# The 65-key score tile of an fp32 attention kernel, computed in column tiles of TensorE's array

## The chip, the cores and the metric

The kernel runs on one core of a Trainium2 chip. Five engines work side by side and meet only at semaphores: TensorE (PE in the profile, with PEld for its weight loads), VectorE (DVE), ScalarE (ACT), GpSimd (POOL) and SyncE (SP, which issues most DMAs). The metric is the device time of one execution in microseconds. Before the change the two runs took 2556.80 and 2558.18 us, median 2557.49 us.

## What is computed

A gated cross-attention block is followed by a gated mixture of low-rank experts, all in fp32. What matters here is the attention, with 4 batches, 256 queries, 1601 keys, 32 query heads in 8 groups of 4 that share keys and values, and head size 128:

```python
q = (query @ Wq + bq).reshape(B, L, NKV, G, HDIM)        # B=4, L=256, NKV=8, G=4, HDIM=128
k_, v_ = jnp.split(kv @ Wkv + bkv, 2, axis=-1)           # 1601 keys
scores = jnp.einsum('blkgd,bmkd->bkglm', q, k) * scale
attn = jax.nn.softmax(scores, axis=-1)
o = jnp.einsum('bkglm,bmkd->blkgd', attn, v).reshape(B, L, NHEAD * HDIM)
return o @ Wo + bo
```

## The kernel before

**Tiles.** The scores are laid out with keys on the partitions and queries along the free dimension. The outer loop runs over the 32 pairs of batch and key head, and within each over two halves `l` of 128 queries: 64 groups. A group has 4 query heads times 128 queries, so 512 query columns (`W`). The 1601 keys are 12 tiles of 128 and one of 65 (`FULL` is the number of that last tile, `REST` is 65). `score_unit(key, j)` computes the scores of one entry of `pairs`: entry 0 is the 65-key tile alone, entries 1 to 6 are two full tiles each. So the 65-key tile opens every group.

**One score tile.** `kT` (128 head dimensions by the keys) is the stationary operand, `qT` (128 by 4 by 128 queries) is streamed, and the result goes to one of the 8 PSUM banks, 512 fp32 columns wide. In the trace each fp32 product stands as two passes, that is two weight loads and two matmul records. ScalarE then copies the bank into the SBUF tile `p` (L1151). `p` has a ring of buffers. A bank or a buffer of `p` can be written again when its reader is done.

**The softmax.** VectorE keeps a running maximum over the group's `p` tiles (`fold`, L1067 to L1073; the 65-key tile joins at L1070, when entry 2 is there). `softmax` reduces it over the partitions and queues the subtraction (VectorE, L1181), the exponential (ScalarE, L1184) and the sums (VectorE, L1073). `av_unit` multiplies the result with the values (L1233). Its first entry again is the 65-key tile, now with 65 rows of contraction.

**The order of the work.** It is written out by a planner at build time: `spend` advances TensorE's planned clock by a product's booked cost, `act` and `vec` those of ScalarE and VectorE, and `pump`, `fit` and `force` take queued pieces of softmax work when the planned clocks allow it. `run_group` puts the score products of one group between the value products of the group before, and `window` fills in projections (L896, L907), output products (L484, L1310) and transposes (L258). The booked costs do not enter the program as such; they only decide in which order each engine's instructions stand. `mm_cost(n)` books 2 * (max(n, 128) / 1.2 + 2) ns for one fp32 product of n columns.

**Two small places elsewhere** that the prediction reads: L238 transposes the biases with 48 rows of contraction, once; L258 transposes the router's weights with 8 rows of contraction, four times near the end. All other products of the kernel contract over 65 or 128 rows and write 65 or 128 partitions.

Of the kernel before, what the change touches and what calls it, by code (L numbers as in the profile page):

```python
# [15 lines left out]
P = 128  # L16
# [3 lines left out]
G = NHEAD // NKV  # L20
# [7 lines left out]
def flamingo_kernel(  # L28
# [51 lines left out]
    nc = tc.nc  # L80
# [8 lines left out]
    FULL = KT - 1 if rows[-1] < P else KT  # L89
    W = G * P  # L90
# [13 lines left out]
    REST = rows[-1] if FULL < KT else 0  # L104
# [13 lines left out]
    SEM = 200  # L118
# [3 lines left out]
    clock = {"now": 0.0, "v": 0.0, "a": 0.0, "hold": 0.0}  # L122
    free = [0.0] * NBANK
    done = {}
    queues = {q: deque() for q in ("sub", "oT", "so", "exp", "ln", "T", "norm", "sum", "low", "low_a")}

    def vec(ns, ready=None):

        clock["v"] = max(clock["v"], clock["now"] + SEM if ready is None else ready) + ns
        return clock["v"] + SEM  # L130

    def act(ns, ready=None):
        clock["a"] = max(clock["a"], clock["now"] + SEM if ready is None else ready) + ns
        return clock["a"] + SEM
# [5 lines left out]
    def start_of(piece):  # L140
        engine, _, ready, _, _ = piece
        if not isinstance(ready, float):
            ready = done.get(ready, NEVER)
        return max(clock[engine], ready)

    def take(q):

        piece = q.popleft()
        engine, ns, _, fn, key = piece
        start = start_of(piece)  # L150
        fn()
        clock[engine] = start + ns
        if key is not None:
            done[key] = start + ns + SEM + (GP_COPIES if key[0] == "part" and key[2] < 4 else 0)

    def pump(until=NEVER, most=None):

        n = 0
        while most is None or n < most:
            heads = [(start_of(q[0]), i, q) for i, q in enumerate(queues.values()) if q]  # L160
            if not heads:
                return n
            start, _, q = min(heads)
            if start == NEVER or start + min(q[0][1], 1200) / 2 > until:
                return n
            take(q)
            n += 1
        return n

    def force(key):  # L170


        while key not in done:
            q = next((q for q in queues.values() if any(p[4] == key for p in q)), None)
            if q is None:

                assert pump(most=1), key
                continue
            ready = q[0][2]
            if not isinstance(ready, float):  # L180
                force(ready)

            engine, start = q[0][0], start_of(q[0])
            for name, other in queues.items():
                fit = 1200 if name == "sub" else FIT
                while other is not q and other and other[0][0] == engine:
                    if start_of(other[0]) + other[0][1] > start + fit:
                        break
                    take(other)
            take(q)  # L190
        return done[key]

    def fit(engine, until):

        while True:
            some = [
                (start_of(q[0]), i, q)
                for i, q in enumerate(queues.values())
                if q and q[0][0] == engine and start_of(q[0]) + q[0][1] <= until + FIT
            ]  # L200
            if not some:
                return
            take(min(some)[2])

    def spend(ns, ready=0.0):

        clock["now"] = max(clock["now"], ready) + ns
        pump(clock["now"])

    def bank(name):  # L210
        free.remove(min(free))
        return ps.tile([P, 512], F32, tag="bank", name=name)

    give = free.append
# [32 lines left out]
    def mm_cost(n):  # L247

        return 2 * (max(n, P) / 1.2 + 2)
# [404 lines left out]
    def key_col(i):  # L654

        return HK if i == FULL else i * P + (REST if i * P >= HK else 0)
# [101 lines left out]
    qT_t, kT_t, v_t = {}, {}, {}  # L758
# [302 lines left out]
    def fold(acc, op, j, key):  # L1061


        p = p_t[key]
        first = NPAIR - FULL // 2
        if j == first + 1:
            nc.vector.tensor_tensor(acc, p[first], p[first + 1], op)  # L1067
            if first:
                r = rows[-1]
                nc.vector.tensor_tensor(acc[:r, 0, :], acc[:r, 0, :], p[0][:r, 0, :], op)  # L1070
                return 1930
        elif j > first + 1:
            nc.vector.tensor_tensor(acc, acc, p[j], op)  # L1073
        else:
            return 0
        return 1220

    def spread(acc, op, nm, res, after=None, eng=nc.vector):
# [31 lines left out]
            (710, back),  # L1110
        ]

    def score_unit(key, j):

        b, h, l = key
        nm = "_".join(map(str, key))
        free_p = 0.0
        if j == 0:
            p_t[key] = []
            acc_t[key] = pool.tile([P, 2, W], F32, tag="mx", name=f"mx_{nm}", bufs=1)  # L1120
        if key == last and j > 0:

            if j == 1:
                flat = pool.tile([P, NC * 2 * HW], F32, tag="ctxT", name="p_last", bufs=1)
                late.extend(
                    flat[:, i * 2 * W : (i + 1) * 2 * W].rearrange("p (t w) -> p t w", t=2)
                    for i in range(NPAIR - 1)
                )
            p = late.pop(0)
        else:  # L1130

            if len(ring) >= NBUF:
                before, i = ring[-NBUF]
                free_p = force(("sum", before, max(i, min(NPAIR - FULL // 2 + 1, NPAIR - 1))))
            ring.append((key, j))
            p = pool.tile([P, 2, W], F32, tag="p", name=f"p_{nm}_{j}", bufs=NBUF)
        p_t[key].append(p)
        for k, i in enumerate(pairs[j]):
            r = rows[i]
            spend(mm_cost(W), max(min(free), done.get(("qT", b, h), 0.0)))  # L1140
            sc = bank(f"sc_{nm}_{i}")
            nc.tensor.matmul(  # L1142
                sc[:r, :],
                kT_t[b, h][:, key_col(i) : key_col(i) + r],
                qT_t[b, h][:, :, l * P : (l + 1) * P],
                start=True,
                stop=True,
            )
            t = max(clock["now"] + SEM, free_p)
            fit("a", t)  # L1150
            nc.scalar.copy(p[:r, k, :], sc[:r, :])  # L1151
            t = act(585, t)
            give(t)
        fit("v", t)
        ns = fold(acc_t[key], ALU.max, j, key)
        if ns:
            vec(ns, t)
# [523 lines left out]
    def run_group(cur, prev, ahead=AHEAD, most=NC * TR_COST):  # L1681


        for j in range(NPAIR + ahead):
            if cur is not None and j < NPAIR:
                score_unit(cur, j)
                if j == NPAIR - 1 and cur[0] == B - 1 and cur[1] >= NKV - 2:
                    softmax(cur)
                short_tasks(most)
            if prev is not None and prev[2] == 0 and j > 2:  # L1690
                block_sums(prev, j >= NPAIR - 1)
            if prev is not None and j >= ahead:
                av_unit(prev, j - ahead)
                short_tasks(most)
        if cur is not None and not (cur[0] == B - 1 and cur[1] >= NKV - 2):
            softmax(cur)
# [173 lines left out]
    for hi, (b, h) in enumerate(heads):  # L1870
        pair, coming = (b, h // 2), next_pair(b, h // 2)
        nxt = heads[hi + 1] if hi + 1 < len(heads) else None
        for l in range(NL):
            now = hi * NL + l
# [99 lines left out]
```

## Time and profile before

| | value |
|---|---|
| runs | 2556.80 and 2558.18 us, median 2557.49 us |
| profiled execution, first to last instruction | 2555.5 us |
| TensorE's granted clock, mean | 1.000 |
| PE busy | 2547.3 us |
| DVE busy | 2202.6 us |
| ACT busy | 1188.1 us |
| 65-key score products (L1142, 128 matmul records) | 65.3 us |
| copies of the 65-key tile (L1151, 64 of them) | 37.2 us |
| mean traffic with HBM | 65 GB/s |

The profile is that of one execution. Busy times are unions, so overlapping records of one engine count once. A matmul record is longer than the distance to the next one because matmuls are pipelined: what a product costs TensorE is the distance between starts, not the length of its record. The profile is read on the engine that has no idle time, and for that engine by its distances.

### The profile page before, as it was taken

What the parts mean: (1) busy time and instruction counts of PE and PEld (TensorE: products, weight loads), DVE (VectorE), ACT (ScalarE), POOL (GpSimd) and SP (SyncE); (2) the same over time, 40 slices, a digit from 0 to 9 for tenths busy, and PEclk for the clock granted to TensorE, in tenths of its full rate; (3) what the DMA queues carried; (4) which work ended last, traced back from release to release, by engine and by line L of the source; (5) the groups of instructions that cost most, each with busy time, mean ns of one, the idle gap of its engine ahead of it and who ended that gap; (6) DMA issues with size and microseconds to landing.
All of it is one profiled execution on the core that took longest, in us unless ns stands there. A gap on an engine that the chain in (4) does not pass through costs nothing.

```text
span 2555.5 us, 26175 instructions
## 1 busy us (share of the span) xinstructions
PE 2547.3 (100%) x9235; PEld 1487.8 (58%) x9235; DVE 2202.6 (86%) x3310; ACT 1188.1 (46%) x1897; POOL 150.4 (6%) x401
## 2 busy tenths in 40 slices
PE   9999999999999999999999999999999999999999
PEld 7557566565555656455565665756656455555554
DVE  4889898899889989899788887878889899998897
ACT  3544454445434555455444444445454445544551
POOL 0000000000000000110000000000000000000000
PEclk9999999999999999999999999999999999999999
DMA  4313222324110111012121111212221011111000
GB/s 158 123 64 108 87 95 84 114 85 149 48 56 23 44 52 56 25 40 83 49 81 37 62 52 62 81 48 81 85 84 56 25 52 52 52 44 52 17 17 33
DMA packets 75499, 167.16 MB, mean 65 GB/s; under 512 B 5372, under 2 KB 32028, under 8 KB 72808
## 3 DMA queue, kind: packets, MB, share of 16 engines
q1 hardware_dynamic: 74424, 164.41, 19.3%
q8 instruction: 73, 1.20, 0.2%
q0 software_dynamic: 416, 0.81, 0.1%
q14 instruction: 58, 0.48, 0.1%
q10 hardware_dynamic: 528, 0.26, 0.0%
HBM read 119.06 MB, written 46.40 MB: 65 GB/s over the span
## 4 chain that ended last, share of the span: by engine, by line
PE 99%; DVE 1%; DMA 0%; ACT 0%; issue 0%; DVEq 0%; ACTq 0%
PE av L1233 28%; PE sc L1142 28%; PE pxk L896 6%; PE pxv L907 6%; PE pxq L896 4%; PE pyk L896 3%; PE pyv L907 3%; PE po L1310 3%; PE pox L484 3%; PE pyq L896 2%; PE pzk L896 2%; PE pzv L907 2%; PE poy L484 1%; PE pzq L896 1%; PE ptv L1020 1%; PE pk L803 1%
## 5 line engine op out<-in xcount | busy, mean ns | idle before, releaser
L1142 PE MATMUL sc<-qT,kT 128*128 128x512 f32 (+1 forms) x1664 | 775.9, 592 | 0.0
L1151 ACT COPY p<-sc 65x512 f32<-65x512 f32 x820 | 474.3, 586 | 636.5 <-PE sc L1142 575.2
L1233 PE MATMUL av<-p,v 65*128 65x512 f32 x1640 | 766.1, 592 | 1.2 <-ACT p L1184 1.2
L1233 PEld LDWEIGHTS av<-p,v 65*128 65x128 f32 x1640 | 309.5, 190 | 376.2 <-issue 370.8
L1142 PEld LDWEIGHTS sc<-qT,kT 128*128 128x128 f32 (+1 forms) x1664 | 307.0, 186 | 374.3 <-issue 340.4
L1181 DVE TENSOR_TENSOR p<-p,mb 65x512 f32<-65x512 f32 x442 | 485.9, 1137 | 0.1
L1184 ACT ACTIVATE p<-p 65x512 f32<-65x512 f32 x442 | 423.1, 990 | 38.6 <-DVE p L1181 34.5
L1073 DVE TENSOR_TENSOR mx<-mx,p 128x1024 f32<-128x1024 f32 x252 | 308.1, 1223 | 137.9 <-ACT p L1151 134.8
L1073 DVE TENSOR_TENSOR sm<-sm,p 128x1024 f32<-128x1024 f32 x252 | 307.4, 1220 | 9.8
L1090 POOL COPY quad_sm<-quad_sm 32x16 f32<-32x16 f32 x186 | 70.7, 380 | 2088.3 <-DVE quad_sm L1086 2083.1
L896 PE MATMUL pxq<-xq,wq 128*128 128x256 f32 x512 | 131.2, 379 | 0.0
L941 ACT ACTIVATE kT<-pxk,biasT 128x384 f32<-128x384 f32 (+1 forms) x120 | 57.9, 508 | 141.8 <-PE pxk L896 141.0
L896 PEld LDWEIGHTS pxq<-xq,wq 128*128 128x128 f32 x512 | 92.5, 189 | 31.2 <-issue 15.3
L941 ACT ACTIVATE qT<-pxq,biasT 128x256 f32<-128x256 f32 x64 | 30.3, 473 | 140.2 <-PE pxq L896 140.2
L944 ACT COPY v<-pxv 128x384 f32<-128x384 f32 x90 | 43.0, 477 | 104.8 <-PE pxv L907 104.8
L896 PE MATMUL pxk<-T,wk 128*128 128x417 f32 (+1 forms) x240 | 90.4, 499 | 0.0
L907 PE MATMUL pxv<-wv,T 128*128 128x128 f32 x720 | 90.2, 275 | 0.0
L896 PE MATMUL pxk<-ctxT,wk 128*128 128x417 f32 (+1 forms) x240 | 90.0, 499 | 0.0
L907 PE MATMUL pxv<-wv,ctxT 128*128 128x128 f32 x720 | 90.0, 275 | 0.0
L907 PEld LDWEIGHTS pxv<-wv,T 128*128 128x128 f32 x720 | 86.4, 192 | 4.7 <-issue 4.3
L907 PEld LDWEIGHTS pxv<-wv,ctxT 128*128 128x128 f32 x720 | 86.4, 192 | 4.7 <-issue 4.3
L1067 DVE TENSOR_TENSOR mx<-p,p 128x1024 f32<-128x1024 f32 x63 | 76.8, 1220 | 13.1 <-ACT p L1151 12.8
(264 smaller groups left out, 2809.6 us busy)
## 6 DMA issues: line engine op xcount, KB each, us to landing
wo<-in_L_xattn_Wo_dram SPq DMA_DIRECT2D x18, 1024.0 KB, 5.3
kept_q<-wq SPq DMA_DIRECT2D x16, 896.0 KB, 4.8
wq<-kept_q SPq DMA_DIRECT2D x16, 896.0 KB, 5.1
wo<-kept_wo SPq DMA_DIRECT2D x13, 1024.0 KB, 5.8
wk<-kept_k SPq DMA_DIRECT2D x11, 896.0 KB, 4.6
wv<-kept_v SPq DMA_DIRECT2D x11, 896.0 KB, 4.4
ctx<-in_ctx_dram SPq DMA_DIRECT2D x36, 256.0 KB, 2.7
wq<-in_L_xattn_Wq_dram SPq DMA_DIRECT2D x32, 256.0 KB, 3.1
```

Of the source, the lines that this page charges most:

```text
L484: nc.tensor.matmul(bk[:, :HD], left[i]()[:, c, :], blk[:, c, :], start=first and c == 0, stop=c == 1, skip_group_check=True,)
L896: nc.tensor.matmul(bk[:, :n], a(SLOT[i], c), operand(i, c, s, n), start=first and c == 0, stop=c == 1, skip_group_check=True,)
L907: nc.tensor.matmul(bk[:, t * HDIM : (t + 1) * HDIM], operand(i, c, s + t * P, P), a(SLOT[i], c), start=first and t == 0 and c == 0, stop=c ...
L941: nc.scalar.activation(dst, src, AF.Identity, bias=bias_of(kind, h0 + f))
L1067: nc.vector.tensor_tensor(acc, p[first], p[first + 1], op)
L1073: nc.vector.tensor_tensor(acc, acc, p[j], op)
L1142: nc.tensor.matmul(sc[:r, :], kT_t[b, h][:, key_col(i) : key_col(i) + r], qT_t[b, h][:, :, l * P : (l + 1) * P], start=True, stop=True,)
L1151: nc.scalar.copy(p[:r, k, :], sc[:r, :])
L1181: nc.vector.tensor_tensor(p, p, m, ALU.subtract)
L1184: nc.scalar.activation(p, p, AF.Exp, scale=scale)
L1233: nc.tensor.matmul(av, v_t[b, h][:r, i, :], p_t[key][j][:r, k, :], start=(j == 0 and k == 0), stop=(j == NPAIR - 1 and k == len(pairs[j]) ...
L1310: nc.tensor.matmul(po, oT_t[key][:, g, :], w_t["o", b, h][:, g, :], start=(g == 0), stop=(g == G - 1),)
```

## The change

The 65-key score tile is no longer one product of 65 keys by 512 queries. Its first 64 keys become two products of 256 queries each. The first writes partitions 0 to 63 of the bank and the second writes partitions 64 to 127, in the same 256 columns. The 65th key becomes four products of one key by 128 queries, which write partitions 0, 32, 64 and 96 of the next 128 columns of the same bank. In the built program the first two have the array shape 128 rows by 64 columns, the other four 128 by 32, and everything around them 128 by 128. Only the last of the six raises the semaphore, by 6.

ScalarE brings the pieces back into the old layout of `p`: two copies of 64 by 256 and four of 1 by 128 in place of one copy of 65 by 512. The first of them waits for all six products. The new function is called from `score_unit` for the tile `FULL`, in all 64 groups.

```diff
+    def split_scores(b, h, l, sc, p, free_p):
+        half, k0 = P // 2, key_col(FULL)
+        kT, qT = kT_t[b, h], qT_t[b, h]
+        for n in range(2):
+            nc.tensor.matmul(
+                sc[n * half : (n + 1) * half, : W // 2],
+                kT[:, k0 : k0 + half],
+                qT[:, 2 * n : 2 * n + 2, l * P : (l + 1) * P],
+                start=True, stop=True, skip_group_check=True,
+            )
+        for g in range(G):
+            nc.tensor.matmul(
+                sc[32 * g : 32 * g + 1, W // 2 : W // 2 + P],
+                kT[:, k0 + half : k0 + half + 1],
+                qT[:, g, l * P : (l + 1) * P],
+                start=True, stop=True, skip_group_check=True, tile_position=(0, 32 * g),
+            )
+        t = max(clock["now"] + SEM, free_p)
+        fit("a", t)
+        for n in range(2):
+            nc.scalar.copy(p[:half, n * W // 2 : (n + 1) * W // 2], sc[n * half : (n + 1) * half, : W // 2])
+            t = act(375, t)
+        for g in range(G):
+            nc.scalar.copy(p[half : half + 1, g * P : (g + 1) * P], sc[32 * g : 32 * g + 1, W // 2 : W // 2 + P])
+            t = act(265, t)
+        return t
...
         for k, i in enumerate(pairs[j]):
             r = rows[i]
+            if i == FULL and REST == P // 2 + 1:
+                spend(mm_cost(W // 2) + mm_cost(P) + 200, max(min(free), done.get(("qT", b, h), 0.0)))
+                sc = bank(f"sc_{nm}_{i}")
+                t = split_scores(b, h, l, sc, p[:, k, :], free_p)
+                give(t)
+                continue
             spend(mm_cost(W), max(min(free), done.get(("qT", b, h), 0.0)))
```

The planner books 848 ns of TensorE for the tile in place of 857, and about 3 us of ScalarE in place of 0.8. So it also places other work differently. On TensorE a few projection and output products change places with their neighbours, on ScalarE and VectorE exponentials, sums and maxima move by some places, and four DMAs move past one neighbour each: three on SP's queue (two copies of query weights to HBM, L337, go ahead of a load of output weights, L424; one load of kept output weights, L421, ahead of another, L375) and one on POOL's (the bias load, L601, ahead of a small copy, L1097). ScalarE loads its function table twice more (once at L287, once at L1184). Apart from these two, no instruction is added or removed but those of the 65-key tile.

## The prediction

> **What bounds the kernel now.** I read the page first, then TensorE's groups by shape, then short stretches of the timeline. The page:
>
> ```profile
> span 2555.5 us, 26175 instructions
> PE 2547.3 (100%) x9235; PEld 1487.8 (58%) x9235; DVE 2202.6 (86%) x3310; ACT 1188.1 (46%) x1897; POOL 150.4 (6%) x401
> PEclk9999999999999999999999999999999999999999
> PE 99%; DVE 1%; DMA 0%; ACT 0%; issue 0%; DVEq 0%; ACTq 0%
> ```
>
> TensorE has no idle time worth the name (2555.5 - 2547.3 = 8.2 us), at full clock, and it is 99% of the chain that ended last. So each nanosecond that the change adds to TensorE's stream shows in the span, and each that it takes away does too, until VectorE (86%) or another engine has to be waited for. The span stands 2.0 us under the median of the runs (2557.49 us); I add the change to the median.
>
> Then the groups by shape: count, busy us, mean record ns, idle before.
>
> ```profile
> L1142 PE MATMUL sc<-qT,kT 128*65 128x512 f32 x128 | 65.3, 592 | 0.0
> L1151 ACT COPY p<-sc 65x512 f32<-65x512 f32 x64 | 37.2, 581 | 58.7 <-PE sc L1142 57.5 <-DVE sm L1073 1.0
> L856 ACT COPY v<-pv 128x256 f32<-128x256 f32 x12 | 3.9, 375 | 11.8 <-PE pv L847 11.8
> L1549 ACT COPY ffn_w<-pmt 128x128 f32<-128x128 f32 x6 | 1.6, 266 | 27.1 <-PE pmt L1544 27.1
> ```
>
> The first is what the change replaces: 64 products in two passes each. A record is 592 ns long, but passes overlap, so their price has to be read as a distance between starts. The timeline gives it (start us, us, what; a run of equal records is one row):
>
> ```profile
> 60.57 1.03 PE L896 MATMUL pxq<-xq,wq 128*128 128x256 f32 x4
> 61.43 1.88 PE L1142 MATMUL sc<-qT,kT 128*65 128x512 f32 x4
> 2395.11 1.50 PE L907 MATMUL pyv<-wv,T 128*128 128x128 f32 x12
> ```
>
> A pass of 512 columns takes (1.88 - 0.592) / 3 = 0.429 us, one of 256 (61.43 - 60.57) / 4 = 0.215, and one of 128 (1.50 - 0.275) / 11 = 0.111, with 0.275 the length of its record. So time goes with the columns streamed, and the weight load beside it is free as long as it is fetched while the pass before streams.
>
> **What the new shapes cost in themselves.** The change leaves the array's 128 x 128 shape in every group. Before does this twice in the whole run, with fewer rows (48 at L238, 8 at L258); with fewer columns it never does.
>
> ```profile
> 9.69 0.60 PE L258 MATMUL pt_ctx<-ident,ctx 128*128 128x128 f32 x4
> 10.21 0.26 PE L238 MATMUL pb<-ident,bias 48*128 48x48 f32 x1
> 10.40 0.66 PE L258 MATMUL pt_ctx<-ident,ctx 128*128 128x128 f32 x4
> ...
> 2417.58 1.02 PE L1142 MATMUL sc<-qT,kT 128*128 128x512 f32 x2
> 2418.53 0.41 PE L258 MATMUL pt_base<-ident,base 8*128 8x8 f32 x4
> 2418.87 1.12 PE L1233 MATMUL av<-p,v 128*128 128x512 f32 x2
> ```
>
> At 9.69 four transposes 0.11 apart should let the next start at 10.12; it starts at 10.21, 0.09 late. That one product then holds the stream 0.19 where 0.06 to 0.11 would do (0.08 to 0.13 too long), and the four after it take 0.66 and not 0.60, because the first had to wait for its own weights (0.06). In all 0.23 to 0.28 us for going in and out. The other place: due at 2417.58 + 2 x 0.429 = 2418.44, started 2418.53 (0.09); its four products are (0.41 - 0.20) / 3 = 0.07 apart, so the last ends its turn at 2418.81 and the next starts at 2418.87 (0.06); and two value passes take 1.12 and not 1.02 (0.10 for exposed weights). In all 0.25. So a change of shape costs 0.06 to 0.13, and the first weights after it 0.06 to 0.10 for 128 columns.
>
> **The sum, part by part.**
>
> *Removed:* two passes of 0.429 = 0.859 us per group.
>
> *Streaming added.* Four passes of 256 and eight of 128. If none lies beside another: 4 x 0.215 + 8 x 0.111 = 1.75 us. If everything that the words promise lies beside each other: 2 x 0.215 + 2 x 0.111 = 0.65. Between them is what I expect. A product's two passes stand next to each other in the stream, records start in the program's order in every row I read, and the second pass of a product uses the same columns of the array as its first. So the first pass of the second column tile can at best run beside the second pass of the first tile, and n tiles take n + 1 slots. That is 3 slots of 0.215 and 5 slots of 0.111: 0.645 + 0.555 = 1.20. Side by side therefore never gets below the 0.859 that it replaces.
>
> *Starting a column tile.* The trace has no two products in different column tiles. The nearest small distance is the 0.07 above; the other end is nothing. There are 1 + 3 such steps per group: 0 to 0.28, I take half, 0.14. The Trainium skill, "TensorE: Matmul & The Clock Gate", section "Measured speedup vs the span model", puts a step between tiles at about 4 ns, which would make this term an estimate of 0.016 and the forecast some 8 us less; no run here shows it.
>
> *Changes of shape:* three per group (into 64 columns, into 32, back to 128). In 0.09 twice, out 0.06 to 0.13, exposed weights 0.10 after the way out and 0.02 to 0.05 after each way in (fewer columns are loaded): 0.34 to 0.51; I take 0.44. The floor for the range is 0, since these rows change the rows of the array and not its columns. The Trainium skill, "TensorEngine Tiling (Array Packing)", section "Tiling Modes", says that changing the mode, not just the tile, drains TensorE; it gives no price, and speaks against a change that does so three times for 65 keys.
>
> *Sum on TensorE:* 1.20 + 0.14 + 0.44 = 1.78 against 0.859: 0.92 us per group, 64 groups, 59 us.
>
> *ScalarE.* Two copies at 375 ns (the 128x256 row) and four at 266 (the 128x128 row) replace one of 581: 2 x 375 + 4 x 266 - 581 = 1233 ns per group, 79 us in all, and two more table loads of 1.28 us. I cost them at nothing: the work that hides them is TensorE's own, since ScalarE is idle 54% of the span and in the row of the 128x512 copies alone waits 517.7 us for scores. Behind the six copies in ScalarE's queue stand the copies of entry 1, and then VectorE's maximum, which takes entry 0 only after entries 1 and 2. With 0.859 per score product and 586 ns per copy, ScalarE regains 0.27 us a tile, more where value products lie between; the bank of the 65-key tile is one of 8. If that cover were gone, up to 79 us would be added.
>
> *The planner.* TensorE is booked 9 ns less, so the plan is near the old one; on SP's queue three DMAs of about 1 MB stand one place earlier, and each lets its neighbour wait for 5 to 6 us (its time to landing); on POOL's the bias load does the same to a small copy. The busiest queue fills 19.3% of the DMA engines, and TensorE waits for none of these in this trace. Price 0, with the 8.2 us of present idle as the scale for either sign.
>
> **Rivals.**
>
> 1. *Nothing runs side by side* (each pass streams alone, whatever its columns). 1.75 + 0.44 = 2.19, +1.33 a group, +85: 2643 us. For it: no row shows two passes in parallel. Against: only the change's own intent, which is no evidence, so I weigh it high.
> 2. *Weights are no longer fetched ahead in column tiles.* Twelve passes each pay 0.05 (half the columns) to 0.10: 2.79 to 3.39, +124 to +162: 2681 to 2720. For: it happens at each change of shape above. Against: in one shape it happens nowhere; the four 8-row products are 0.07 apart.
> 3. *Everything side by side, shape changes priced as above:* 0.65 + 0.44 = 1.09, +15: 2572 us.
> 4. *The other side: everything side by side and shape changes free.* 0.65 against 0.859, 0.20 us saved a group: 2544 us. It decides where three changes cost less than 0.20 together, 0.07 each; the two rows say 0.06 to 0.13 plus weights, and the order of the passes speaks against it too.
> 5. *ScalarE becomes late,* and entry 0's copies hold up banks: up to 79 us on top of the forecast, 2696. Against: its idle time above.
>
> **How the numbers follow.** Forecast 2557.5 + 59 = 2617 us, chance 0.56. Its own range: low with 0 and 0.34 (1.54, +44: 2601), high with 0.28 and 0.51 (1.99, +72: 2630). Rival 1 has 0.22, rival 2 0.07, rival 3 0.08, rival 4 0.05, rival 5 0.02. The range of 2572 to 2646 holds the forecast and rivals 1 and 3, also side by side in order with free changes of shape (1.20, +22); it leaves out rivals 2, 4 and 5, 0.14, and what little lies outside the forecast's own range. A difference of 2%, about what a measurement of this kernel can tell from no change, is 51 us, or 1.66 us for the new tile. Seven tenths of the forecast's cases lie above that, all of rivals 1, 2 and 5, none of 3 and 4: 0.39 + 0.31 = 0.70, which I lower to 0.67 since the border runs through the likeliest case. Faster by 2% would need 0.80 of the 0.859 us saved: 0.01. Within 2%: 0.32.
>
> **What would show it.** In the trace after: the first pass of the second 256-column product starting with the second pass of the first (0.22 after the start, not 0.43) shows the staggered order; four single-key products taking 0.56 and not 0.89 show the same. The wait ahead of the first 64-column pass, of the first single-key pass and of the next full product's second pass give the three changes. ScalarE's busy time should rise by some 80 us with TensorE's idle time still near 8 us; if that rises by tens, rival 5 was right. I am wrong if the distance from the first split pass to the next full score pass is not between 1.5 and 2.0 us.

## The result, and the profile after

The changed kernel takes 2577.59 us (2576.85 and 2578.32), 20.1 us more than before: ratio 1.0076, 95% interval 1.0047 to 1.0105. The forecast was 2617 us. So it is slower, as forecast, but by a third of the forecast amount. It lies inside the stated range of 2572 to 2646 us only because that range also held rival 3; the forecast's own range began at 2601, and slower by more than 2%, to which I had given 0.67, did not come (it is 0.8%).

The page of the kernel after, the lines that answer to those shown of before:

```profile
span 2575.1 us, 27764 instructions
PE 2563.0 (100%) x9875; PEld 1485.5 (58%) x9875; DVE 2205.2 (86%) x3310; ACT 1259.8 (49%) x2219; POOL 144.7 (6%) x401
PE 99%; DVE 1%; ACT 0%; DMA 0%; issue 0%; SPq 0%; ACTq 0%; DVEq 0%
```

The span grew by 19.6 us. TensorE's busy time grew by 15.7 us of this, and its idle time by the rest (2575.1 - 2563.0 = 12.1 us, 8.2 before). These are two separate effects. The first is in the new tile. Its groups by shape, and one group in the timeline:

```profile
L1118 PE MATMUL sc<-qT,kT 128*64 128x256 f32 x256 | 41.7, 405 | 0.0
L1125 PE MATMUL sc<-qT,kT 128*1 128x128 f32 x512 | 25.6, 271 | 0.0
...
1504.55 0.81 PE L484 MATMUL pox<-xa,xa 128*128 128x256 f32 x3
1505.29 0.65 PE L1118 MATMUL sc<-qT,kT 128*64 128x256 f32 x4
1505.87 0.40 PE L1125 MATMUL sc<-qT,kT 128*1 128x128 f32 x8
1506.20 1.56 PE L1176 MATMUL sc<-qT,kT 128*128 128x512 f32 x3
```

In the last four rows the first number is the start in us, the second the time to the end of the row's last record. Read as in the prediction, by distances. The three output passes (`pox`) start 0.215 apart, the last at 1504.98, so the next is due at 1505.19; it starts at 1505.29. Four passes of 256 columns then lie within 0.65 us, of which 0.38 is the length of the last record. So the last one started only 0.27 after the first; four in a row would have put it at 0.65 or later. The eight single-key passes start within 0.40 - 0.27 = 0.13. From the first split pass to the next full one it is 0.91 us (1506.20 - 1505.29). I had set 1.5 to 2.0 as the bounds outside of which I would be wrong.

The exact record starts are the same to a few ns in all 64 groups. I call *tile time* the distance from when the first split pass was due to where the next full product would have started with its weights ready (the start of its second pass less 0.4295 us). Its median is 1.109 us; before it was 0.859:

| piece of the tile time | us |
|---|---|
| late start of the first split pass | 0.093 |
| two slots of 256 columns | 0.431 |
| weights of the first pass, not fetched ahead | 0.052 |
| from 64 columns to 32, beyond the slot | 0.100 |
| two slots of 128 columns | 0.216 |
| from 32 columns to 128, beyond the slot | 0.113 |
| weights of the next full product | 0.104 |

The three changes of shape have one price. Counted from where the last pass of the old shape ends its slot, in whichever column tile it is, the next pass starts 0.093 us later in all three; the 0.100 and 0.113 hold besides it the one and the three steps of 0.007 by which the last column tile started behind the first. In all ten profiles with narrow shapes this price is 0.093 to 0.095 (medians).

64 x (1.109 - 0.859) = 16.0 us. This is, to 0.3 us, the growth of TensorE's busy time. The other 4 us are in the list of what TensorE waited for (engine, line, what for: us, times, longest):

```profile
PE av L1267 <- ACT p L1218: 3.3, 2, 1.6
PE sc L1176 <- ACT p L1185: 1.4, 1, 1.4
PE warm L1829 <- DVE ones L1826: 1.1, 1, 1.1
PE pt_ctx L258 <- DMA ctx<-in_ctx_dram: 1.0, 1, 1.0
```

Before, the corresponding list had one wait for an exponential and none for a score copy:

```profile
PE av L1233 <- ACT p L1184: 1.2, 1, 1.2
```

Two waits on ScalarE are new. One is a value product that waits for an exponential (1.63 us at 2490.58), the other a score product that waits for a bank (1.43 us at 1105.53).

### The profile page after: what moved, and what is told of

The parts are those of the page before. It is cut to its first block, busy times and chain, and to the rows that moved or that the text cites. A ratio compares the mean times of both kernels' runs of the same rounds, so it can differ in the third digit from the quotient of the medians.

```text
span 2575.1 us, 27764 instructions
## 1 busy us (share of the span) xinstructions
PE 2563.0 (100%) x9875; PEld 1485.5 (58%) x9875; DVE 2205.2 (86%) x3310; ACT 1259.8 (49%) x2219; POOL 144.7 (6%) x401
## 4 chain that ended last, share of the span: by engine, by line
PE 99%; DVE 1%; ACT 0%; DMA 0%; issue 0%; SPq 0%; ACTq 0%; DVEq 0%
PE av L1267 28%; PE sc L1176 26%; PE pxv L907 6%; PE pxk L896 6%; PE pxq L896 4%; PE po L1344 3%; PE pyk L896 3%; PE pyv L907 3%; PE pox L484 3%; PE pyq L896 2%; PE pzk L896 2%; PE pzv L907 2%; PE sc L1118 1%; PE poy L484 1%; PE pzq L896 1%; PE ptv L1020 1%
## 5 line engine op out<-in xcount | busy, mean ns | idle before, releaser
L1176 PE MATMUL sc<-qT,kT 128*128 128x512 f32 x1536 | 727.8, 597 | 1.4 <-ACT p L1185 1.4
L1185 ACT COPY p<-sc 128x512 f32<-128x512 f32 x756 | 431.3, 588 | 519.6 <-PE sc L1176 445.3
L1176 PEld LDWEIGHTS sc<-qT,kT 128*128 128x128 f32 x1536 | 284.8, 190 | 346.5 <-issue 315.8
```

The source lines that it names most:

```text
L1176: nc.tensor.matmul(sc[:r, :], kT_t[b, h][:, key_col(i) : key_col(i) + r], qT_t[b, h][:, :, l * P : (l + 1) * P], start=True, stop=True,)
```

## The experiments

The theory after the result: passes in different column tiles stream together whenever their tiles are free, so the tile streams for 0.65 us and pays 0.46 for three changes of shape; the other 4 us come from the order of other work or from ScalarE's extra copies. Each experiment takes one of these apart. The diffs are against the changed kernel; `...` stands for lines left out. Times are medians, each beside runs of before on the same chip (median 2557.3 to 2558.5 us). Tile times are read from the record starts as above.

### Same width, one column tile (same_tile)

```diff
-                sc[n * half : (n + 1) * half, : W // 2],
+                sc[:half, n * W // 2 : (n + 1) * W // 2],
...
-                sc[32 * g : 32 * g + 1, W // 2 : W // 2 + P],
+                one[:1, g * P : (g + 1) * P],
...
-                start=True, stop=True, skip_group_check=True, tile_position=(0, 32 * g),
+                start=True, stop=True, skip_group_check=True, tile_position=(0, 0),
```

`one` is a second bank; the copies, left out here, read from the new places.

> All six products of the 65-key tile stay as narrow as in the changed kernel, but every one goes to the first column tile of its shape (two banks instead of one). Theory, side by side: what makes the changed tile 1.11 us is that passes in different column tiles stream together (0.65 us) while three changes of shape cost 0.46. Without different tiles the passes stream one after another: 4 x 0.215 + 8 x 0.111 = 1.75, with 0.46 it is 2.21 us a group, 1.35 over the old tile, +87, with some 4 us of waits about 2648 us. Rival, narrow passes are cheap in themselves, whichever tile they lie in: the time stays at 2578 us.

2640.83 us, ratio 1.0326 (1.0311 to 1.0341). The timeline of one group:

```profile
865.12 1.08 PE L1118 MATMUL sc<-qT,kT 128*64 128x256 f32 x4
866.12 1.03 PE L1125 MATMUL one<-qT,kT 128*1 128x128 f32 x8
867.09 0.70 PE L1178 MATMUL sc<-qT,kT 128*128 128x512 f32 x1
```

The same four passes now take 1.08 us where they lay within 0.65, and the eight take 1.03 where they lay within 0.40. The tile time is 2.169 us, and 64 x (2.169 - 0.859) = 83.8 us against 83.5 measured. So the narrow passes are not cheaper in themselves here; it takes different column tiles for them to share the array. The expectation of 2648 us was 7 too high: 2.6 us is in the tile (2.21 for 2.169), and the new waits on ScalarE, 4 us, did not come in this run. This is also what the prediction's first rival would have looked like (2643 us).

### The order of the products (order)

```diff
         for n in range(2):
-            nc.tensor.matmul(
-                sc[n * half : (n + 1) * half, : W // 2],
-                kT[:, k0 : k0 + half],
-                qT[:, 2 * n : 2 * n + 2, l * P : (l + 1) * P],
+            for g in range(2):
+                nc.tensor.matmul(
+                    sc[n * half : (n + 1) * half, g * P : (g + 1) * P],
+                    kT[:, k0 : k0 + half],
+                    qT[:, 2 * n + g, l * P : (l + 1) * P],
...
```

> The 64 keys as four products of 128 queries: two in the first column tile, then two in the second. Theory, passes of different tiles are brought together however far apart they stand in the program: 4 x 0.111 = 0.44 for the four products, as much as the two of 256 take now: 2578 to 2580 us. Rival, only products that are neighbours in the program share the array: of the eight passes at most one pair lies side by side, 7 x 0.111 = 0.78, +0.35 a group over the changed kernel, +22: 2600 us; with none side by side 8 x 0.111 = 0.89, +29: 2607 us.

2579.09 us, ratio 1.0084 (1.0069 to 1.0099), tile time 1.121. In the group that starts at 845.08 the eight 64-column passes start at 0, 0.014, 0.160, 0.174, 0.269, 0.283, 0.379 and 0.392: four pairs. The two products for the second tile stand behind both products for the first in the program, and still each of their passes goes beside one of the first tile's. So two products need not be neighbours in the program to share the array.

### One shape less (two64)

```diff
-        for g in range(G):
+        for n in range(2):
             nc.tensor.matmul(
-                sc[32 * g : 32 * g + 1, W // 2 : W // 2 + P],
-                kT[:, k0 + half : k0 + half + 1],
-                qT[:, g, l * P : (l + 1) * P],
+                sc[n * half : (n + 1) * half, W // 2 :],
+                kT[:, k0 + half : k0 + 2 * half],
+                qT[:, 2 * n : 2 * n + 2, l * P : (l + 1) * P],
...
```

The four copies of the 65th key, left out here, read from the new places.

> The 65th key is computed in the 64-column shape as well: a slice of 64 keys that starts with it (the other 63 rows are not used) by 256 queries in each of the two column tiles. One change of shape fewer. Theory: 2 x 0.215 + 2 x 0.215 streaming, in 0.093 + 0.052, out 0.113 + 0.104: 1.22 us a group, 0.36 over the old tile, +23, with 4 us of waits 2585 us. Rival, the 0.10 us ahead of the single-key products is not the change of shape but theirs whatever the shape (new weights, another part of the bank): 1.32 us, 2591 us.

2588.26 us, ratio 1.0120 (1.0105 to 1.0135).

```profile
1312.74 0.65 PE L1118 MATMUL sc<-qT,kT 128*64 128x256 f32 x4
1313.22 0.60 PE L1125 MATMUL sc<-qT,kT 128*64 128x256 f32 x4
```

The time, 3 us from either forecast, does not tell the two apart; the tile time does. It is 1.211, as expected by the theory (1.22) and not by the rival (1.32). The pairs start at 0, 0.267, 0.483 and 0.699: the last key's pairs follow at the plain slot of 0.216. So the 0.100 ahead of the single keys in the changed kernel belongs to the change from 64 to 32 columns. The tile explains 22.5 of the 30.9 us. TensorE's idle time explains most of the rest: 2586.9 - 2571.8 = 15.1 us in this profile, 6.9 more than before, with 3.5 us of waiting for loads of the context at the start in it (1.0 in the changed kernel). What is left, some 2 us, is open.

### Everything in 32 columns (one32)

```diff
+        def part(tile, k, m, g0, n, at):
+            nc.tensor.matmul(
+                sc[32 * tile : 32 * tile + m, at * P : (at + n) * P],
+                kT[:, k0 + k : k0 + k + m],
+                qT[:, g0 : g0 + n, l * P : (l + 1) * P],
+                start=True, stop=True, skip_group_check=True, tile_position=(0, 32 * tile),
+            )
+        part(0, 0, 32, 0, 3, 0)
+        part(1, 32, 32, 0, 3, 0)
+        part(2, 0, 32, 3, 1, 0)
+        part(3, 32, 32, 3, 1, 0)
+        part(2, 64, 1, 0, 2, 1)
+        part(3, 64, 1, 2, 2, 1)
```

These six stand in place of the two loops over products; ScalarE's copies, left out here, become four.

> The whole tile in the 128 x 32 shape: keys 0 to 31 and 32 to 63 by three heads in tiles 0 and 1 (384 columns), the fourth head in tiles 2 and 3 (128 columns), then the 65th key by two heads in tiles 2 and 3 (256 columns). Each tile streams 384 columns, two changes of shape, four copies on ScalarE. Theory, tiles stream independently: 2 x 0.322 + 0.36 = 1.01 us, 0.15 over the old tile, +9 to +14: 2567 to 2571 us. Rival, tiles only share the array with the product next to them and of the same length: 2 x 0.322 + 2 x 0.111 + 2 x 0.215 = 1.30 and 0.36: 1.66 us, +51 to +55: 2608 to 2612 us.

2570.95 us, ratio 1.0056 (1.0039 to 1.0073); tile time 0.985, and 64 x 0.126 = 8.1 us of the 13.6. TensorE's idle time, 12.2 us in this profile, is 4.0 more than before; the profiled execution took 2569.38 us, 1.6 less than the median. In the timeline, all twelve passes and the next full product:

```profile
843.35 0.86 PE L1118 MATMUL sc<-qT,kT 128*32 128x384 f32 x12
844.13 0.70 PE L1178 MATMUL sc<-qT,kT 128*128 128x512 f32 x1
```

The twelve lie within 0.86 us; one after another their columns alone would take some 4 x 0.32 + 4 x 0.111 + 4 x 0.215 = 2.6. Tiles 2 and 3 start their single-key passes at 0.256 while tiles 0 and 1 are still in their first pass; their second starts at 0.347. So each tile goes on with its own next pass whatever the others do.

### Who puts them side by side (late_b)

```diff
+        late = qT[:, 2:3, l * P : l * P + 1]
+        nc.scalar.copy(late, late)
         for n in range(2):
             nc.tensor.matmul(
                 sc[n * half : (n + 1) * half, : W // 2],
```

> The changed kernel, with one ScalarE copy of one column of the third head's queries onto itself ahead of the split products, so that the second 64-key product must wait for ScalarE while the first does not. In groups where ScalarE is late the order of the four passes tells who put them side by side. Theory, the array takes the passes as they become free: while the second product waits, the first one's second pass starts 0.27 us after its first pass, ahead of the second product's first pass. Rival, the passes were set in the order first-first, first-second before the run: the first product's second pass never starts ahead of the second product's first, however late that is. Time: 2578 us plus what TensorE waits for ScalarE, at most some 0.6 us a group, 2578 to 2616 us, by either.

2609.23 us, one run. ScalarE was late in 46 of 64 groups. In 40 of them the first product's second pass had started by then (at 0.27 us), and the second product started only 0.58 to 1.35 us after the first. In one of these groups the weight loads, and then TensorE's passes up to 0.6 us into the group, read:

```profile
212.21 0.19 PEld L1120 LDWEIGHTS sc<-qT,kT 128*64 128x64 f32 x2
212.94 0.19 PEld L1120 LDWEIGHTS sc<-qT,kT 128*64 128x64 f32 x2 [0.54 <-ACT qT L1118]
...
212.21 0.65 PE L1120 MATMUL sc<-qT,kT 128*64 128x256 f32 x2
```

Both passes of the first product are under way at 212.21 (the second starts 0.65 - 0.38 = 0.27 after the first), while the second product waits until 212.94. In six groups ScalarE was only a little late, and the order turns. Here the same stretch of another group, cut 0.15 and 0.35 us after its start:

```profile
170.65 0.55 PE L1120 MATMUL sc<-qT,kT 128*64 128x256 f32 x2
...
170.65 0.65 PE L1120 MATMUL sc<-qT,kT 128*64 128x256 f32 x3
```

The second record to start does so at 0.55 - 0.43 = 0.12 and is a first pass (0.43 long, with its weights not fetched ahead); the third starts at 0.65 - 0.38 = 0.27 and is the first product's second pass. So here the second product's first pass goes ahead of the first product's second pass; in the 40 groups it came behind it. In the six groups it starts 0.04 to 0.25 us after the first record, and in the other 18, where ScalarE was not late, 0.007. The same program gives both orders, depending on when a semaphore came. So the order is made at run time, and each row fits one account: a pass starts when its tile is free and its own wait is over. The rival, an order set before the run, is out.

### The order of the other work (new_plan, old_plan)

The old tile with the new bookings, and the new tile with the old bookings. In the first diff the one old product, left out here, also takes the place of the six:

```diff
-            nc.scalar.copy(p[:half, n * W // 2 : (n + 1) * W // 2], sc[n * half : (n + 1) * half, : W // 2])
-            t = act(375, t)
...
+        nc.scalar.copy(p[:r, :], sc[:r, :])
+        for ns in (375, 375, 265, 265, 265, 265):
+            t = act(ns, t)
```

```diff
-                spend(mm_cost(W // 2) + mm_cost(P) + 200, max(min(free), done.get(("qT", b, h), 0.0)))
+                spend(mm_cost(W), max(min(free), done.get(("qT", b, h), 0.0)))
...
-            t = act(375, t)
...
-            t = act(265, t)
-        return t
+        return act(585, t)
```

> The old tile (one product, one copy), with the planner's bookings of the changed kernel, so that only the order of the other work is new. Theory, the change of 20 us is 16 us in the tile itself and 4 us of waits on ScalarE: 2557 to 2561 us, the upper end if the waits come from the new order. Rival, the new order costs most of it: 2570 to 2577 us.

> The changed tile with the bookings of the old one, so that the order of the other work is the old order. Theory: the 16 us of the tile stay; 2574 us if the 4 us of waits come from the new order, 2578 us if they come from ScalarE's six copies. Rival, order costs most: 2560 us.

new_plan: 2561.58 us, ratio 1.0012 (1.0003 to 1.0022), 3.1 us over before. old_plan: 2573.97 us, ratio 1.0061 (1.0048 to 1.0074), 15.5 us over before, against 16.0 from its tile times. The two parts make 18.6 of the 20.1 us, the whole within their intervals (0.8 to 5.6 and 12 to 19 us). The new order alone brings the new waits, without any split product; it is in this list of what TensorE waited for in new_plan:

```profile
PE av L1254 <- ACT p L1205: 2.8, 2, 1.6
PE sc L1163 <- ACT p L1172: 1.7, 2, 1.4
```

and the old order, with all six copies, has neither the second value wait nor the bank wait (here old_plan, the first two rows):

```profile
PE av L1265 <- ACT p L1216: 1.6, 1, 1.6
PE warm L1827 <- DVE ones L1824: 1.1, 1, 1.1
```

TensorE's idle time in old_plan is 2571.9 - 2563.3 = 8.6 us, against 8.2 before. So the six copies cost next to nothing as work. What cost 3 to 4 us is the order that the planner made from the new bookings, in which the copies stand with 3 us of ScalarE (the 9 ns less of TensorE were not tried alone).

### Without the 65th key (pair_only)

```diff
-        for g in range(G):
-            nc.tensor.matmul(
-                sc[32 * g : 32 * g + 1, W // 2 : W // 2 + P],
...
-            nc.scalar.copy(p[half : half + 1, g * P : (g + 1) * P], sc[32 * g : 32 * g + 1, W // 2 : W // 2 + P])
+            nc.scalar.copy(p[half : half + 1, g * P : (g + 1) * P], sc[32 * g : 32 * g + 1, :P])
```

> Leaves out the four products of the 65th key; its row of p is filled by the same four copies from scores of other keys. Theory: 2 x 0.215 and one way in and out (0.36) are 0.79 us a group, 0.07 less than the old tile, -4 us, with up to 4 us of waits: 2553 to 2557 us. Rival, the changed tile is dear because ScalarE has six copies for one: 2570 us or more, since the copies are all still there.

2557.16 us, ratio 0.9996 (0.9988 to 1.0005).

```profile
1294.78 0.65 PE L1118 MATMUL sc<-qT,kT 128*64 128x256 f32 x4
1295.36 1.55 PE L1169 MATMUL sc<-qT,kT 128*128 128x512 f32 x3
```

The tile time is 0.780, so 64 x 0.079 = 5.1 us are saved, TensorE's busy time is 2542.8 us (4.5 less than before), and the waits of the new order give most of it back (TensorE's idle time is 12.6 us). Two halves side by side gain 0.43 us and the way in and out takes back 0.35. The 65th key costs 0.33 more (0.216 streaming and 0.11 for its own shape).

### Fewer changes of shape (batch, batch32)

Both halves of a head are computed when the first begins; the second half's bank is held until its group. batch uses the shapes of the changed kernel, batch32 those of one32. `split_products`, left out here, holds the products of both halves.

```diff
+                if l == 0:
+                    spend(2 * (mm_cost(W // 2) + mm_cost(P)) + 400, max(min(free), done.get(("qT", b, h), 0.0)))
+                    for l_ in range(NL):
+                        held[l_] = bank(f"sc_{b}_{h}_{l_}_{i}")
+                    split_products(b, h)
+                t = split_scores(b, h, l, held.pop(l), p[:, k, :], free_p)
```

> The changed tile for both halves of a head at once, at the start of the first half; the second half's scores wait in their bank until that half begins. Three changes of shape per head instead of six. Theory, the changes of shape are what the changed kernel pays: 2 x 0.65 + 0.46 = 1.77 us per head against 1.72 of the old tile, +2 us, with waits up to 4: 2559 to 2563 us. Rival, a bank held for a whole group is missed: TensorE waits for banks, 2570 us or more.

> Both halves of a head at once, and all in the 128 x 32 shape (three slots of 128 columns per tile and half): two changes of shape per head. Theory, if tiles stream independently: 4 x 0.322 + 0.36 = 1.65 us per head against 1.72 of the old tile, -4 to -2 us, with waits up to 4: 2554 to 2559 us. Rival, unequal lengths do not pack: 2 x 1.30 + 0.36 = 2.96 us per head, +40: 2597 us.

batch: 2560.91 us, ratio 1.0013 (1.0004 to 1.0022), 1.759 us per head, that is 0.880 per tile. batch32: 2555.55 us, ratio 0.9994 (0.9985 to 1.0003), 1.634 us per head, 0.817 per tile; TensorE is busy for 2545.1 us, 2.2 less than before. One head of batch32, all 24 passes:

```profile
838.74 1.51 PE L1121 MATMUL sc<-qT,kT 128*32 128x384 f32 x24
```

In neither profile does TensorE wait longer than 0.4 us for an exponential or a score copy, so a bank held for a group is hardly missed. batch is 16.7 us faster than the changed kernel. The changes of shape, half as many, are 64 x (1.109 - 0.880) = 14.7 of it; most of the rest are the waits, which this order of the work does not have. With one shape it ends 1.8 us below before. That this is faster than before is not shown: the interval includes 1.

## Why the prediction was wrong, point by point

- *TensorE bounds the kernel and each nanosecond on it shows.* Right. The tile times explain the measured times to 0.5 us where the plan is the old one (old_plan) or TensorE hardly waits (same_tile).
- *Streaming, 1.20 us.* This is the step that failed. I wrote that "records start in the program's order in every row I read" and that therefore "the first pass of the second column tile can at best run beside the second pass of the first tile, and n tiles take n + 1 slots". The rows of before could not show otherwise, since all but five of its products and transposes are in one shape, and not one is in a column tile. late_b and order show that passes start out of the program's order across column tiles, and same_tile that two tiles are what it takes; measured 0.65 us, the bottom end of my bounds. The difference, 0.55 us in 64 groups, is 35 us of the 39 that I was off.
- *Starting a column tile, 0.14 us.* Too much, by 7 us in 64 groups. Neighbouring tiles start 0.007 us apart (0.014 in order, where another product stands between the two): the 1 + 3 steps are 0.03 us, and they stand in the tile time as what its 0.100 and 0.113 have above 0.093. I had taken half of 0.07 from a row that shows one tile being loaded again. The Trainium skill, "TensorE: Matmul & The Clock Gate", section "Measured speedup vs the span model", has about 4 ns; this trace has 7, and 0.007 is what holds here.
- *Changes of shape, 0.44 us.* Right: 0.46 (0.093 + 0.052 + 0.100 + 0.113 + 0.104). Two single places in the trace, at which rows and not columns changed, gave the price; that it carried over to columns was not known before. The same 0.093 on the way in stands in every one of the 64 groups. The sum of the low bound is off: its own terms (0.18 + 0.06 + 0.10 + 0.04) make 0.38 and not 0.34, which moves the forecast's low end from 2601 to 2604 and changes nothing else.
- *ScalarE's copies at nothing.* Right as work: its busy time rose by 71.7 us (1188.1 to 1259.8; I had 79 and 2.6 for the table loads), TensorE's idle time by 3.9.
- *The planner at nothing, on a scale of 8.2 us.* Small but not nothing: 3.1 us in new_plan, within that scale.
- *The rivals.* Rival 3 (all side by side, shape changes as priced: 2572 us) was what happened, with the 4 us of the new order on top. I gave it 0.08. Rival 1 is what same_tile shows and rival 2 is what no run shows: weights were not fetched ahead only for the first pass of each tile after a change of shape.
- *2% as about what a measurement can tell.* Too coarse: the interval of the result is 0.3% to either side, and those of the experiments are narrower.

## What to carry to other kernels

In these runs, all of fp32 products over 128 rows, column tiles share the array fully, whatever the order and length of the products tried, so streaming is the columns of the busiest tile; but each way into a narrower shape and back took 0.35 us, and an in-between shape 0.1 more. Split a narrow product only if it saves more columns than that (an estimate: at 0.859 us for 512 columns, 0.35 us is about 200 columns of an fp32 product), and put several such products behind one another before going back. Since passes start out of the program's order, mind which product raises the semaphore: in every kernel here the passes of the program's last products also start last, and a program in which an earlier product ends later was not run. Before pricing two operations as sequential because no row shows them together, look whether any row could have shown it; and a changed cost in a planner is a change of its own, best tried without the work it stands for.

## What the runs showed of the hardware

- TensorE starts passes out of the program's order across column tiles. In late_b, from one program, the second pass to start is the first product's second in 40 groups and the second product's first in 24; in one32 a product that is last in the program starts 0.09 us before the second pass of the first.
- Passes of 128 and 384 columns in different tiles need no common slot (one32: 0.985 us with 0.645 of it for the busiest tile's columns).
- A change of the array's shape (the five ways tried: 128 to 64 or 32 columns, 64 to 32, and from both back) delays the next pass by 0.093 to 0.095 us after the last pass of the old shape. The first weights after it are exposed by about their columns: 0.026 us for 32 (one32), 0.052 for 64, 0.104 for 128.
